# Lists of places made in pieces behind the table chunks, place loads split from their subtraction, and transposed rows kept in the tiles of the sums

## The chip, the core and the metric

The kernel runs on one core of a Trainium2 chip. The core has five engines that run their own instruction streams and meet at semaphores: PE (TensorE, the matrix unit), DVE (VectorE), ACT (ScalarE), POOL (GpSimd, here used to start gathers of table rows) and SP (SyncE, here used to start transfers). ACT also starts transfers. Sixteen DMA engines move the data between the memory of the chip and the on-chip buffers SBUF and PSUM. The metric is the device time of one execution in microseconds (us); lower is better.

## The reference

One step of message passing on a graph with 12,500 nodes of 64 values and 200,000 edges of 32 values. The edges are sorted by destination.

```python
msg_in = jnp.concatenate([nodes[row], nodes[col], edge_features], axis=-1)
messages = relu(msg_in @ mW1 + mb1) @ mW2 + mb2
aggregated = jax.ops.segment_sum(messages, col, num_segments=nodes.shape[0])
upd_in = jnp.concatenate([nodes, aggregated], axis=-1)
x = layernorm(x + relu(upd_in @ uW1 + ub1) @ uW2 + ub2)
```

`row` is the source of an edge and `col` its destination. The hidden width is 128.

## The kernel before, in words

The first matrix mW1 is split into the rows for the source, for the destination and for the edge values. Two tables are made once, A = x times the source rows and B = x times the destination rows, both with 12,500 rows of 128 values in the memory of the chip. An edge then needs one row of A (its source), one row of B (its destination) and a small product of its 32 own values.

**Opening: 13 chunks.** Table A is made in 13 chunks of 8 blocks of 128 nodes (the last has 2 blocks). For chunk k, `chunk_a` lets PE multiply the blocks into a PSUM buffer `pb`; ACT copies one half of it to an SBUF tile `tb` (L656), DVE the other half (L654), and ACT then starts the store of `tb` to table A (L658). There are two `pb` buffers and four `tb` buffers, so PE can start chunk k+2 when both halves of chunk k are copied, and the copies of chunk k+4 wait until the store of chunk k has landed. Between the chunks stand other pieces of work: one chunk of table B, the comparison masks of the first edge groups (`select_rows`, L273, and `select`, L281), and, behind chunk 10, `offsets()`. This function makes, on one partition, the lists of places at which the sums of each edge tile are to be added: `usup`, `woff`, `wcnt` and `ustep`, views of one tile `lists`. They are read by PE's sequencer in `collect`, from step 1 on. POOL starts gathers during the chunks: 48 gathers of rows of x for the first eight steps (a batch of four is held until ACT has copied the chunk ahead of it), and gathers of table A only after all 13 stores have landed.

**The steps.** The edges are worked in 261 steps of 6 tiles of 128 edges. In step s, PE adds the source rows to a PSUM tile `pc` (`node_part`), ACT or DVE applies relu into `h`, PE adds the counts and the messages of step s-1 into the running sums (`collect`, L486 and L490), and makes the part of the destinations and edge values of step s+1 (`edge_part`, L410). `pc` takes the same two PSUM buffers that the chunks used as `pb`. For the first eight steps the source rows come from x itself, not from table A: PE transposes them (`transpose`, L326) into one PSUM tile `pt`, ACT copies them to a tile `xt` (L327) and `node_part` multiplies them by the source matrix (L429). `xt` is a buffer of the same rotation of four as `tb`. From step 8 on rows of table A are gathered and added (L437). The order of instructions on each engine is the order in which the program is written; nothing reorders it.

**Relative places.** In steps 1, 2 and 3 `rest(s)` calls `relative(a, b)`: SP starts a load of 512 columns of destinations (`dst`, L599) and of the first destination of each tile (`wrow`, broadcast to all partitions into `col_a`, L600), and DVE subtracts one from the other (L601) into `drc`. `col_a` is one buffer, so the second load waits for the first subtraction. `drc` beyond its first 96 columns is read by `select` from step 13 on.

**Tiles of the sums.** `sums_s[0]` and `sums_s[1]` are two SBUF tiles that take the finished sums of a stretch of nodes; the first of them is written behind step 44, where the first stretch of 45 steps ends.

Of the kernel before, what the change touches and what calls it, by code (L numbers as in the profile page):

```python
# [10 lines left out]
F32 = mybir.dt.float32  # L11
I32 = mybir.dt.int32
AF = mybir.ActivationFunctionType
ALU = mybir.AluOpType
# [3 lines left out]
P = 128  # L18
# [5 lines left out]
NT = -(-E // P)  # L24
SUB = 6
SUP = 12
NSUP = -(-NT // SUP)
NTP = NSUP * SUP
# [44 lines left out]
U8 = mybir.dt.uint8  # L73
YBASE = XBASE + 4 * XCOLS
LEAD = 8
SBASE = (33556480, 33554432)
CBASE = 33566720
PACE = ((11, 0.48), (50, 0.505), (130, 0.483), (170, 0.469), (261, 0))
# [49 lines left out]
def gnn_kernel(ctx: ExitStack, tc: tile.TileContext, x1T, x, eT, e_rows, src, src_row, dst, dst_row, wlist, wrow, wnext, whalf,  # L128
# [117 lines left out]
    with tc.tile_pool(name="work", bufs=2) as work, tc.manual_schedule():  # L246
# [74 lines left out]
        def transpose(s):  # L321

            a = xg.pop(s)[1]
            xt = work.tile([P, SUB // 2, P], F32, name="xt", tag="tb", bufs=4)
            for k in range(SUB // 2):
                nc.tensor.transpose(pt[:, k, :], a[:, 2 * k:2 * k + 2].rearrange("p k d -> p (k d)"), ident)  # L326
            nc.scalar.copy(xt, pt)  # L327
            xs[s] = xt
# [264 lines left out]

        WCH = 512

        def relative(a, b):

            wbc = col_a.rearrange("p a e b -> p (a e b)")[:, :b - a]
            nc.sync.dma_start(dst_s[:, a:b], dst[:, a:b])  # L599
            nc.sync.dma_start(wbc, wrow[:, a:b].broadcast_to([P, b - a]))  # L600
            nc.vector.tensor_tensor(drc[:, a:b], dst_s[:, a:b], wbc, op=ALU.subtract)  # L601

        def halves(a, b):

# [64 lines left out]
        def offsets():  # L669

            nc.vector.memset(usup[:, 0:1], 0)
            wv = wint.rearrange("o (s t) -> o s t", t=LS)
            ov = woff.rearrange("o (s t) -> o s t", t=LS)
            k, runs = 0, []
            while k < K:
                end = UPD[k + 1:] + [NSUB]
                d = end[0] - UPD[k]
                n = 1
                while k + n < K and k and end[n] - UPD[k + n] == d:
                    n += 1  # L680
                if k:
                    nc.vector.tensor_copy(usup[:, k:k + n], wv[:, UPD[k]:UPD[k] + (n - 1) * d + 1:d, 0])
# [4 lines left out]
                k += n  # L687
            nc.vector.tensor_tensor(ustep[:, 1:], usup[:, 1:], usup[:, :-1], op=ALU.subtract)
            for v in (woff[:, :NSUB * LS], ustep[:, 1:]):
                nc.vector.tensor_scalar(v, v, 0.0, float(UN), op0=ALU.max, op1=ALU.min)  # L690
            v = woff[:, :NSUB * LS]
            nc.vector.tensor_scalar(wcnt[:, :NSUB * LS], v, 4.0, float(CBASE), op0=ALU.mult, op1=ALU.add)
            nc.vector.tensor_scalar(v, v, 4.0, float(SBASE[0]), op0=ALU.mult, op1=ALU.add)
            for k, d, n in runs:
                if k % 2 == 0:
                    k, n = k + 1, n - 1
                if n > 0:
                    o = ov[:, UPD[k]:UPD[k] + n * d].rearrange("o (n d) t -> o n (d t)", n=n)[:, ::2]
                    nc.vector.tensor_scalar(o, o, float(SBASE[1] - SBASE[0]), None, op0=ALU.add)

        dst_s = drc.bitcast(I32)
        nc.scalar.dma_start(src_s[:, :64], src[:, :64])
# [32 lines left out]
        for r in rhs:  # L735
            for o in EK:
                nc.sync.dma_start(r[o:o + DE], mW1[2 * D:, :].unsqueeze(1).broadcast_to([DE, SUP // 2, DH]))
        for k, c in enumerate(range(0, NB, NCH)):
            copied = chunk_a(c)
            for i, u in enumerate(first[:EACH]):  # L740
                fetch(u, None if i else copied)
            first = first[EACH:]
            if k == 2:
                chunk_b(0, [B0v, Bv])
            if k == 3:
                nc.vector.tensor_tensor(drc[:, :8 * SUP], dst_s[:, :8 * SUP], early, op=ALU.subtract)
                first_nodes(0, 8)
            if k == 4:

                w0 = wint[:, :GE * SUP // SUB * LS]  # L750
                nc.vector.tensor_scalar(past, w0[:, GE * SUP // SUB * LS - 1:], float(EARLY - WIN), None, op0=ALU.is_gt)
                nc.vector.tensor_scalar(w0, w0, float(EARLY - WIN), None, op0=ALU.min)
                windows(0)
                windows(1)
            if k in (5, 7):
                g = (k - 5) // 2
                select_rows(g)
                load(g)
                select(g)
                counts(g)  # L760
            if k == 10:
                offsets()
        assert not first

        def rest(s):
# [370 lines left out]
```

## Time and profile before

| what | value |
|---|---|
| runs of the kernel (three) | 2145.4, 2143.6, 2152.13 us |
| median | 2145.4 us |
| profiled execution, whole time | 2147.86 us |
| its span from first to last instruction | 2146.1 us |
| mean granted TensorE clock | 0.778 |
| opening until PE starts the first step | 80.09 us |
| PE starts the node part of step 15 at | 213.47 us |
| from there to the end of the span | 1932.53 us |

Rows of the timeline give the start in us, the duration in us, the engine, the source line, the operation, output and input, the number of merged instructions, and in brackets the idle time of the engine just before and what ended it. `ACTq` and `SPq` rows are starts of transfers. "issue" means that the engine waited for nothing that the profile shows, "remote" that the release is not among the instructions shown. The ends of matrix multiplications are modelled. A row of the view by stretches gives, for each engine, busy time and number of instructions, then the granted clock of PE, the share of the DMA engines and the transfer rate.

### The profile page before, as it was taken

The page shows a single profiled execution, that of the slowest core. Times are in us where ns is not written, and L with a number is a line of the kernel's source. Part 1 is how long each engine was busy: PE and PEld are TensorE (multiplying, and loading weights), DVE is VectorE, ACT ScalarE, POOL GpSimd, SP SyncE. Part 2 cuts the span into 40 slices and gives each one's busy share as a digit, 9 for nine tenths or more (in the row PEclk, how much of TensorE's full clock was granted, in tenths as well). Part 3 has the DMA queues.
Part 4 walks back from the last instruction along what each step waited for, and adds up shares of the span by engine and source line. Part 5 has one row for each costly group of instructions (what it writes and reads, how often), then busy time and mean ns, then how long its engine had stood idle before and what let it go on. Part 6 is the DMA issues. An engine that isn't in the chain of part 4 may idle for free. (4 is left out here: it accounts for less than half of the span.)

```text
span 2146.1 us, 47795 instructions
## 1 busy us (share of the span) xinstructions
PE 1692.0 (79%) x10742; PEld 1284.5 (60%) x10742; DVE 1135.8 (53%) x8047; ACT 1575.1 (73%) x8029; POOL 1257.7 (59%) x1336
## 2 busy tenths in 40 slices
PE   3476877888778887878887887888887888888888
PEld 3454665666555665656565656556665666666666
DVE  2414555565555555565555645565555565555553
ACT  1155988769869697889677877787877877878872
POOL 6565666665666666555656655565656666666650
PEclk8667877777787778787877777787788787878788
DMA  8452333332222222232223323233333333333331
GB/s 221 114 138 73 104 89 97 89 92 74 78 74 78 75 79 79 76 85 78 76 81 83 89 75 88 81 94 83 81 89 85 84 96 85 92 86 94 85 89 40
DMA packets 207836, 190.41 MB, mean 89 GB/s; under 512 B 57909, under 2 KB 174093, under 8 KB 207549
## 3 DMA queue, kind: packets, MB, share of 16 engines
q0 software_dynamic: 42464, 85.48, 16.0%
q1 hardware_dynamic: 150396, 92.86, 15.5%
q10 hardware_dynamic: 14690, 8.99, 1.5%
q8 instruction: 90, 1.47, 0.3%
q14 instruction: 196, 1.61, 0.2%
HBM read 169.15 MB, written 18.02 MB: 87 GB/s over the span
## 5 line engine op out<-in xcount | busy, mean ns | idle before, releaser
L239 POOL DMA_INDIRECT xg<-tab_a,src_s x1279 | 1211.0, 947 | 806.7 <-issue 264.7
L381 ACT ACTIVATE xc<-xtop,xbot 128x1 f32 x7872 | 1491.8, 293 | 163.6 <-issue 118.8
L389 DVE TENSOR_TENSOR xc<-xtop,xbot 128x1 int32 x7232 | 607.0, 155 | 470.6 <-issue 455.4
L490 PE MATMUL sums<-band,h 128*128 128x96 f32 x3126 | 539.2, 327 | 144.0 <-issue 88.4
L490 PEld LDWEIGHTS sums<-band,h 128*128 128x128 f32 x3126 | 476.8, 233 | 174.3 <-issue 103.4
L437 PE MATMUL pc<-xg,band 128*128 128x384 f32 (+1 forms) x1008 | 451.5, 574 | 31.8 <-issue 26.7
L410 PE MATMUL pc<-rhs,l 64*128 64x128 f32 x3126 | 371.5, 351 | 89.7 <-issue 66.3
L410 PEld LDWEIGHTS pc<-rhs,l 64*128 64x128 f32 x3126 | 291.8, 234 | 140.5 <-issue 97.5
L450 DVE TENSOR_SCALAR h<-pc 128x768 f32<-128x768 f32 x252 | 240.3, 953 | 197.2 <-PE sums L490 69.5
L437 PEld LDWEIGHTS pc<-xg,band 128*128 128x128 f32 x1008 | 216.4, 237 | 148.8 <-issue 96.3
L273 DVE TENSOR_TENSOR l<-l,cps 128x768 f32<-128x768 int32 (+1 forms) x134 | 127.1, 948 | 146.0 <-PE pc L437 66.8
L486 PEld LDWEIGHTS <-one 128*1 128x1 bf16 x1563 | 56.5, 81 | 215.3 <-issue 211.0
L561 ACT ACTIVATE y<-cps 128x256 f32<-128x256 f32 (+1 forms) x36 | 13.7, 382 | 179.8 <-issue 86.9
L486 PE MATMUL cnt<-band,one 128*1 128x32 bf16 x1563 | 89.6, 180 | 42.2 <-issue 40.9
L544 ACT ACTIVATE hTu<-sums,ub_s 128x416 f32<-128x416 f32 (+1 forms) x36 | 21.7, 603 | 96.0 <-PE pc L437 23.8
L413 PE MATMUL pc<-band,xc 64*128 64x128 f32 x472 | 77.6, 313 | 17.3 <-issue 16.7
L281 DVE TENSOR_TENSOR band<-cps,drc 128x384 f32<-128x384 f32 x131 | 71.7, 547 | 22.1 <-remote 14.9
L646 PE MATMUL pb<-band,xtop 64*128 64x128 f32 x200 | 43.7, 386 | 41.8 <-DVE tb L654 27.2
L413 PEld LDWEIGHTS pc<-band,xc 64*128 64x128 f32 x472 | 64.0, 228 | 15.5 <-issue 15.4
L646 PEld LDWEIGHTS pb<-band,xtop 64*128 64x128 f32 x200 | 38.3, 281 | 46.7 <-DVE tb L654 28.6
L239 POOL DMA_INDIRECT xg<-in_x,src_s x48 | 45.7, 952 | 24.3 <-issue 13.1
L552 PE MATMUL cps<-ux,xw 128*128 128x64 f32 x284 | 54.3, 347 | 5.2 <-issue 5.0
(107 smaller groups left out, 657.5 us busy)
## 6 DMA issues: line engine op xcount, KB each, us to landing
l<-in_dst_row SPq DMA_DIRECT2D x262, 96.0 KB
l<-in_eT SPq DMA_DIRECT2D x262, 96.0 KB
xg<-tab_a,src_s POOLq DMA_INDIRECT x1279
rhs<-tab_b SPq DMA_DIRECT2D x361, 32.0 KB
tab_b<-tb SPq DMA_DIRECT2D x13, 512.0 KB
rhs<-tab_b SPq DMA_DIRECT2D x387, 16.0 KB
tab_a<-tb ACTq DMA_DIRECT2D x12, 512.0 KB
out<-y SPq DMA_DIRECT2D x35, 128.0 KB
```

The source lines that it names most:

```text
L239: ins = nc.gpsimd.indirect_dma_start(out=a[:, i, :] if s < XG else a[:, i // 2, i % 2, :], out_offset=None, in_=A[:, :] if s >= XG else x[ ...
L273: nc.vector.tensor_tensor(l[r], l[r].bitcast(I32), node[r].unsqueeze(2).broadcast_to([r.stop - r.start, SUP // 2, P]), op=ALU.is_equal)
L281: nc.vector.tensor_tensor(s[:, :nt], slot.unsqueeze(1).broadcast_to([P, nt, WIN]), drc[:, g * SUP:g * SUP + nt].unsqueeze(2).broadcast_to( ...
L381: nc.scalar.activation(o[:, e:e + 1], top.bitcast(F32), AF.Identity, bias=bot.bitcast(F32))
L389: nc.vector.tensor_tensor(o[:, e:e + 1].bitcast(I32), top.bitcast(I32), bot.bitcast(I32), op=ALU.bitwise_or)
L410: done = nc.tensor.matmul(pc[:, b, k, :], L[g][q:q + 64, m, :], rhs[g % 2][q:q + 64, w, :], start=k == 0, stop=False)
L413: done = nc.tensor.matmul(pc[:, b, k, :], xc[s][q:q + 64], w1a[q:q + 64], start=False, stop=False)
L437: added = nc.tensor.matmul(pc[:, b, :m], ident, a[:, b, :m], start=False, stop=True)
L450: nc.vector.tensor_scalar(h, pc, 0.0, None, op0=ALU.max)
L486: nc.tensor.matmul(pn8[:, bass.ds(cs[i] - CBASE, 4 * WIN)].bitcast(F32), one, SB[g][:, k0 + i, :, 1], start=False, stop=ends and i == n - 1)
L490: made.append(nc.tensor.matmul(ps8[:, bass.ds(ws[i] - SBASE[u % 2], 4 * WIDE * WIN)].bitcast(F32), h[:, i % 2, i // 2, :], widened(g, k0 + i),
L646: nc.tensor.matmul(pb[:, h, i, :], (xbot if h else xtop)[64 * h:64 * h + 64, (c + HB * h + i) * P:(c + HB * h + i + 1) * P], w[64 * h:64 * ...
```

## The change

Three edits, all in the opening and the first eight steps.

1. `offsets()` becomes a generator that yields after each piece, and behind each of the chunks 5 to 12 up to four pieces are taken. The pieces are the same instructions in the same order.
2. `relative` is split. `absolute_load` starts the two loads in steps 1, 3 and 5; `relative`, now only the subtraction, runs in steps 3, 5 and 7, ahead of the next load into the same buffer.
3. `transpose` writes its copy into `sums_s[s % 2]` instead of a buffer of the rotation that the table chunks use.

```diff
+OFFS = 4
 def transpose(s):
     a = xg.pop(s)[1]
-    xt = work.tile([P, SUB // 2, P], F32, name="xt", tag="tb", bufs=4)
+    xt = sums_s[s % 2][:, :SUB // 2 * P].rearrange("p (k n) -> p k n", n=P)
...
+def absolute_load(a, b):
+    nc.sync.dma_start(dst_s[:, a:b], dst[:, a:b])
+    nc.sync.dma_start(col_a.rearrange("p a e b -> p (a e b)")[:, :b - a], wrow[:, a:b].broadcast_to([P, b - a]))
 def relative(a, b):
-    wbc = col_a.rearrange("p a e b -> p (a e b)")[:, :b - a]
-    nc.sync.dma_start(dst_s[:, a:b], dst[:, a:b])
-    nc.sync.dma_start(wbc, wrow[:, a:b].broadcast_to([P, b - a]))
-    nc.vector.tensor_tensor(drc[:, a:b], dst_s[:, a:b], wbc, op=ALU.subtract)
+    nc.vector.tensor_tensor(drc[:, a:b], dst_s[:, a:b], col_a.rearrange("p a e b -> p (a e b)")[:, :b - a],
+                            op=ALU.subtract)
...
 # in offsets(): a yield after each run of stretches, after ustep, after each clamp,
 # after wcnt, after woff, and after every fourth of the last additions
...
+places_made = offsets()
 for k, c in enumerate(range(0, NB, NCH)):
     copied = chunk_a(c)
...
-    if k == 10:
-        offsets()
+    if k > 4:
+        for _ in range(OFFS):
+            next(places_made, None)
+for _ in places_made:
+    pass
...
-    if 1 <= s < 4:
-        relative(8 * SUP + (s - 1) * WCH, min(8 * SUP + s * WCH, NT))
-        if s == 2:
-            halves(4 * SUP, NTP // 2)
+    for stage, a in ((relative, s - 3), (absolute_load, s - 1)):
+        if a in (0, 2, 4):
+            stage(8 * SUP + a // 2 * WCH, min(8 * SUP + (a // 2 + 1) * WCH, NT))
+    if s == 2:
+        halves(4 * SUP, NTP // 2)
```

Where the lists stand on DVE, before: `tb_356`, `tb_373` and `tb_390` are the halves of chunks 8, 9 and 10, and the whole of `offsets()` begins behind them.

```order
L654 COPY tb_356<-pb_347 128x512
L654 COPY tb_373<-pb_364 128x512
L654 COPY tb_390<-pb_381 128x512
L671 MEMSET usup_104 1x1
L684 TENSOR_TENSOR lists_69<-lists_69,usup_104 1x360
L682 COPY usup_104<-lists_69 1x1
```

The same place on DVE after the change: `tb_380` and `tb_401` are the halves of chunks 8 and 9.

```order
L688 TENSOR_TENSOR lists_69<-lists_69,usup_104 1x48
L658 COPY tb_380<-pb_371 128x512
L693 TENSOR_TENSOR ustep_105<-usup_104 1x35
L696 TENSOR_SCALAR lists_69<-lists_69 1x2088
L696 TENSOR_SCALAR ustep_105<-ustep_105 1x35
L699 TENSOR_SCALAR lists_69<-lists_69 1x2088
L658 COPY tb_401<-pb_392 128x512
L701 TENSOR_SCALAR lists_69<-lists_69 1x2088
L708 TENSOR_SCALAR lists_69<-lists_69 1x152
```

The 12 differences (L688), which stood between chunks 10 and 11, are now behind chunks 5, 6 and 7, four behind each; four instructions stand behind chunk 8 and the last ten behind chunk 9, so that the halves of chunks 10 and 11 follow each other on DVE with nothing between.

On DVE in the first steps, before: the subtractions of `relative` (L601) stand behind the half of chunk 11 (`tb_441`) and the masks of the third group, in the steps whose `rest` starts their loads.

```order
L654 COPY tb_441<-pb_432 128x512
L273 TENSOR_TENSOR l2_82<-l2_82,cps_101 32x768 x2
L281 TENSOR_TENSOR band_97<-cps_101,drc_102 128x384
L601 TENSOR_TENSOR drc_102<-drc_102,col_a_71 128x512 x2
L273 TENSOR_TENSOR l0_80<-l0_80,cps_101 128x768
```

The same stretch of DVE after the change: the subtractions are L604.

```order
L658 COPY tb_441<-pb_432 128x512
L274 TENSOR_TENSOR l2_82<-l2_82,cps_101 32x768 x2
L282 TENSOR_TENSOR band_97<-cps_101,drc_102 128x384
L274 TENSOR_TENSOR l0_80<-l0_80,cps_101 128x768
L282 TENSOR_TENSOR band_97<-cps_101,drc_102 128x384
L604 TENSOR_TENSOR drc_102<-drc_102,col_a_71 128x512
```

The first subtraction now stands behind the masks of the fourth group, two steps behind its own load, and the next two follow one group of masks later each. On SP the loads of the second and third pieces move from steps 2 and 3 to steps 3 and 5.

On ACT in the same stretch, before, with the semaphores that each instruction waits for (names with DMAHW count landed transfers):

```order
L656 COPY tb_448<-pb_445 128x256 [waits DMAHW7_49,PE_49]
L658 DMA tab_a_63<-tb_448 128x2x128 [waits DMAHW5_49,Activation_49]
L327 COPY xt_451<-pt_117 128x384 [waits DMAHW2_49,PE_49]
L431 ACTIVATE h_480<-pc_456 128x768 [waits PE_49]
L327 COPY xt_490<-pt_117 128x384 [waits DMAHW3_49,PE_49]
L431 ACTIVATE h_504<-pc_495 128x768 [waits PE_49]
L327 COPY xt_556<-pt_117 128x384 [waits DMAHW4_49,PE_49]
```

And after the change:

```order
L660 COPY tb_448<-pb_445 128x256 [waits DMAHW1_49,PE_49]
L662 DMA tab_a_63<-tb_448 128x2x128 [waits Activation_49]
L328 COPY sums_s0_73<-pt_117 128x384 [waits PE_49]
L432 ACTIVATE h_479<-pc_455 128x768 [waits PE_49]
L328 COPY sums_s1_74<-pt_117 128x384 [waits PE_49]
L432 ACTIVATE h_502<-pc_493 128x768 [waits PE_49]
L328 COPY sums_s0_73<-pt_117 128x384 [waits PE_49,Activation_49]
```

The copies of the transposed rows stand at the same places and no longer wait for a landed transfer. From step 10 on the order on all engines is the same as before.

More of the change, by code (lines that the diff above doesn't have):

```diff
@@ L687, in offsets @@
                 k += n
+                yield
             nc.vector.tensor_tensor(ustep[:, 1:], usup[:, 1:], usup[:, :-1], op=ALU.subtract)
+            yield
             for v in (woff[:, :NSUB * LS], ustep[:, 1:]):
                 nc.vector.tensor_scalar(v, v, 0.0, float(UN), op0=ALU.max, op1=ALU.min)
+                yield
             v = woff[:, :NSUB * LS]
             nc.vector.tensor_scalar(wcnt[:, :NSUB * LS], v, 4.0, float(CBASE), op0=ALU.mult, op1=ALU.add)
+            yield
             nc.vector.tensor_scalar(v, v, 4.0, float(SBASE[0]), op0=ALU.mult, op1=ALU.add)
+            yield
             for k, d, n in runs:
@@ L699, in offsets @@
                     nc.vector.tensor_scalar(o, o, float(SBASE[1] - SBASE[0]), None, op0=ALU.add)
+                    if k % 4 == 0:
+                        yield
         dst_s = drc.bitcast(I32)
```

## The prediction

> **What bounds the kernel now.** I read the page first, then the view by stretches, then the timeline of each engine over the opening.
>
> ```profile
> span 2146.1 us, 47795 instructions
> PE 1692.0 (79%) x10742; PEld 1284.5 (60%) x10742; DVE 1135.8 (53%) x8047; ACT 1575.1 (73%) x8029; POOL 1257.7 (59%) x1336
> ```
>
> ```profile
> 60.00:80.00 20.00, 4.99 (x39) 4.40 (x39) 13.89 (x42) 1.76 (x3) 9.01 (x10) 0.59 0.40 103
> ...
> 600.00:800.00 200.00, 163.12 (x977) 121.26 (x975) 111.21 (x862) 166.53 (x879) 121.71 (x129) 0.77 0.29 78
> ```
>
> Over the long run of steps PE and ACT are each over 80% busy (163.12 and 166.53 of 200 us), and PE at a granted clock of 0.77. The opening is another stage: in 60 to 80 us PE works 4.99 of 20 us, and DVE is the busiest engine with 13.89. The change touches only the opening and the first eight steps, so I look for what ends last there and ask how far a shift lasts.
>
> ACT and DVE between chunk 7 and the first steps:
>
> ```profile
> 56.16 0.59 ACT L656 COPY tb<-pb 128x512 f32<-128x512 f32 x1 [14.39 <-remote]
> ...
> 61.08 0.59 ACT L656 COPY tb<-pb 128x512 f32<-128x512 f32 x1 [2.53 <-DVE tb L654]
> ...
> 64.80 0.59 ACT L656 COPY tb<-pb 128x512 f32<-128x512 f32 x1 [3.13 <-PE pb L646]
> 66.14 0.37 ACTq L658 DMA_DIRECT2D tab_a<-tb  x1
> 74.08 0.59 ACT L656 COPY tb<-pb 128x512 f32<-128x512 f32 x1 [8.69 <-remote]
> 80.07 0.37 ACTq L658 DMA_DIRECT2D tab_a<-tb  x1
> 80.54 0.37 ACT L656 COPY tb<-pb 128x256 f32<-128x256 f32 x1 [5.87 <-DVE tb L654]
> 80.94 0.37 ACTq L658 DMA_DIRECT2D tab_a<-tb  x1
> 81.40 0.48 ACT L327 COPY xt<-pt 128x384 f32<-128x384 f32 x1 [0.49 <-ACT tb L656]
> ...
> 97.42 0.48 ACT L327 COPY xt<-pt 128x384 f32<-128x384 f32 x1 [9.27 <-remote]
> ```
>
> ```profile
> 41.81 0.69 DVE L654 COPY tb<-pb 128x512 f32<-128x512 f32 x1 [1.80 <-issue]
> 56.78 0.69 DVE L654 COPY tb<-pb 128x512 f32<-128x512 f32 x1 [14.28 <-ACT tb L656]
> ...
> 59.43 0.56 DVE L281 TENSOR_TENSOR band<-cps,drc 128x384 f32<-128x384 f32 x1
> 59.91 0.68 DVE L654 COPY tb<-pb 128x512 f32<-128x512 f32 x1
> 61.70 0.69 DVE L654 COPY tb<-pb 128x512 f32<-128x512 f32 x1 [1.11 <-issue]
> 65.42 0.69 DVE L654 COPY tb<-pb 128x512 f32<-128x512 f32 x1 [3.02 <-issue]
> 66.05 0.06 DVE L671 MEMSET usup<- 1x1 int32 x1
> ...
> 70.07 0.43 DVE L682 COPY usup<-lists 1x4 int32<-1x4 int32 x1
> ...
> 73.92 0.18 DVE L688 TENSOR_TENSOR ustep<-usup 1x35 int32<-1x35 int32 x1 [0.50 <-issue]
> ...
> 76.87 1.24 DVE L693 TENSOR_SCALAR lists<-lists 1x2088 int32<-1x2088 int32 x1
> ...
> 79.35 0.69 DVE L654 COPY tb<-pb 128x512 f32<-128x512 f32 x1
> ...
> 92.60 0.69 DVE L601 TENSOR_TENSOR drc<-drc,col_a 128x512 f32<-128x512 int32 x1 [10.01 <-issue]
> 97.22 0.69 DVE L601 TENSOR_TENSOR drc<-drc,col_a 128x512 f32<-128x512 int32 x1 [3.92 <-DMA col_a<-in_wrow]
> ...
> 118.28 0.62 DVE L601 TENSOR_TENSOR drc<-drc,col_a 128x443 f32<-128x443 int32 x1 [14.36 <-DMA col_a<-in_wrow]
> ```
>
> ```profile
> 57.53 0.58 PE L646 MATMUL pb<-band,xtop 64*128 64x128 f32 x1 [12.89 <-DVE tb L654]
> ...
> 60.64 0.58 PE L646 MATMUL pb<-band,xtop 64*128 64x128 f32 x1 [1.03 <-DVE tb L654]
> ...
> 62.51 0.51 PE L646 MATMUL pb<-band,xtop 64*128 64x128 f32 x1
> ...
> 80.09 1.65 PE L410 MATMUL pc<-rhs,l 64*128 64x128 f32 x12 [12.75 <-DVE tb L654]
> ...
> 89.79 0.49 PE L326 MATMUL pt<-band,xg 128*128 128x128 f32 x3
> ...
> 97.95 1.65 PE L429 MATMUL pc<-band,xt 64*128 64x128 f32 x12 [6.80 <-issue]
> ```
>
> ```profile
> 70.81 0.95 POOL L239 DMA_INDIRECT xg<-in_x,src_s  x1 [0.30 <-issue]
> 84.58 0.95 POOL L239 DMA_INDIRECT xg<-tab_a,src_s  x1 [12.82 <-DMA tab_a<-tb]
> ```
>
> DVE takes its half of chunk 10 at 65.42, works on the lists from 66.05 on, and takes its half of chunk 11 at 79.35. ACT's half of chunk 11 was copied at 74.08 to 74.67. ACT can't start the store before DVE is done (80.07), chunk 12 stands behind it (80.54, 80.94), PE's first step waits for the same PSUM buffer (80.09, 12.75 us idle ahead of it), and POOL waits 12.82 us for all stores until 84.58. So the lists hold the end of the opening, but only from 74.67 on: before that DVE would have waited for ACT, and ACT for something the profile calls remote (8.69 us).
>
> **The lists in pieces.** The instructions are the same; their time on DVE is 66.05 to 79.35, 13.3 us. By the rows above, the pieces behind chunks 5 and 6 end at 70.07 (4.0 us); those behind chunk 7 reach to 73.92 (3.85, with small idle times), behind chunk 8 to 76.87 (2.95), behind chunk 9 to 79.35 (2.5). The first 4.0 us are free: chunk 6's half ends at about 42.5 us, and DVE then idles 14.28 us ahead of 56.78. The rest stands between the halves of chunks 7 to 10. From DVE's 59.99 (end of the masks behind chunk 7): pieces to 63.8, chunk 8's half to 64.5 (60.6 before), pieces to 67.5, chunk 9's half to 68.1 (62.4 before), pieces to 70.6, chunk 10's half to 71.3 (66.1 before). So three stores start 4 to 6 us later, at 64.5, 68.1 and 71.3; nobody waits for these alone, since POOL needs all 13. ACT comes to chunk 11 at 71.8, by the 0.47 us from 80.07 to 80.54.
>
> When is chunk 11's product there for ACT? This the trace doesn't show, as the release at 74.08 has no name, so I bound it. Early end: PE's chunk 11 starts when chunk 9's half is copied (62.51 now, 68.2 then) and takes as long as chunk 10 did, from 60.64 to ACT's copy at 64.80, 4.2 us; that is 72.4, then 0.59 for ACT and 0.69 for DVE, and the store starts at 73.7, which is 6.4 us earlier than 80.07. Late end: it takes as long from its start as it did itself, 74.08 less 62.51, 11.6 us; that is 79.8, the store starts at 81.1, 1.0 us later than now. I take the time at which it came, 74.08: it lies between the two, and the wait ended 2.3 us after POOL's last gather of the opening (70.81 and 0.95), whose batch is released by chunk 7's copy (56.16), and that doesn't move. Then DVE's half ends at 75.4 and the store starts there: **4.6 us earlier**, with ends of 6.4 earlier and 1.0 later. PE's first step starts with it, and POOL's gathers of table A, by the 3.64 us from 80.94 to 84.58, at about 80.0.
>
> **The subtractions apart from their loads.** DVE waits 10.01, 3.92 and 14.36 us for these loads (rows 92.60, 97.22, 118.28). Behind it on DVE stand the masks of the groups that PE reads three steps later; SP's next loads wait for those masks:
>
> ```profile
> 93.32 0.33 SPq L600 DMA_DIRECT2D col_a<-in_wrow  x1
> ...
> 98.80 0.81 SPq L294 DMA_DIRECT2D l<-in_eT  x2
> ```
>
> The broadcast at 93.32 waited 4 us for the first subtraction; it goes. The edge values loaded at 98.80 belong to group 3, which is steps 6 and 7, and PE is then at the node part of step 2 (97.95), so what DVE and SP gain here ends as idle time. Nothing is late next: the three subtractions of 0.69, 0.69 and 0.62 us run in steps 3, 5 and 7, when their loads are long there, and are read from step 13 on. The same two times 256 KB per piece move, the second and third piece later. I count 0; if the transfers at 93 to 97 us slowed what PE waited for, it is part of the larger case below.
>
> **The transposed rows in the tiles of the sums.** The first copy at 81.40 follows chunk 12's store start by 0.46 us, so it hardly waited for a buffer. The third, at 97.42, waited 9.27 us, and PE with it (97.95; its transposes ran at 89.79 to 90.28). Its buffer was that of chunk 11's store. But POOL, which waits for that very store, went on at 84.58, so the store had landed 13 us before; I count 0 for this edit as well. Bounds: a gain of 97.42 less 90.28, 7.1 us, if the wait is the buffer's after all, and no loss, as the copy has the same shape and only waits for less.
>
> [...]
>
> **The sum.** 4.6 and 0 and 0: 4.6 us off 2147.86 gives 2143.3 us for the profiled execution. That execution is 2.46 us above the median of 2145.4, so I forecast **2140.8 us**. That the gain stays to the end I take from the code: from step 10 on all engines have the same order, no step waits for a fixed time, and each is released by the one before.
>
> **The rivals.**
> - *No lag at chunk 11.* ACT's wait for it goes with the new order, and the early end holds: 6.4 us, 2139.0. For it speak chunks 9 and 10 (57.53 to 61.08 and 60.64 to 64.80); against it that ACT had no work and still waited 8.69 us.
> - *The buffer was the wait.* The third copy runs at PE's pace: 4.6 and 7.1, 2133.7. For it speaks that the copy at 97.42 came 0.2 us after a transfer had landed for DVE (97.22); against it POOL's row.
> - *Slower: chunk 11 hangs on its own start.* The pieces behind chunks 7 and 8 push PE's start of chunk 11 from 62.51 to 68.2, and if it then needs 11.6 us the store starts at 81.1. This costs 1.0 us: 2146.4. It decides from a start of 67.2 on; the reckoning has 68.2. The 8.69 us without work between speak for a lag of PE, the 4.2 us of chunk 10 against it.
> - *Slower: the granted clock answers.* PE starts 4.6 us sooner and has fewer pauses, and is granted less. Clock rows of one run go from 0.59 to 0.77 by stretch. A hundredth of 0.77 over the 1692 us that PE is busy is 22 us, more than the whole gain; it decides from two thousandths on, and gives some 2163 with a hundredth. Against it: after step 10 the work is the same.
>
> **How the numbers follow.** Likeliest 0.46; no lag 0.12; the buffer 0.19; slower by chunk 11 0.15; slower by the clock 0.08. What a measurement can tell from no change I put at 0.5%, 10.7 us, from the spread of the three runs (2143.6 to 2152.13). Only the buffer's case passes it on the fast side (11.7 us) and the clock's on the slow side: faster 0.19, same 0.73, slower 0.08. The range holds the first four cases, with 2133.7 and 2146.4 as its ends, and some us for the spread of runs above: 2132 to 2149. What is left out is the clock's 0.08 and a part of the buffer's case.
>
> **What would show it.** Right: DVE's half of chunk 11 starts straight behind ACT's, at about 74.7; the store at 75.4; POOL's first row of table A at 80; no L604 with more than 1 us of idle ahead; the third transposed copy still some 7 us behind its transposes. Wrong: chunk 11's copy on ACT at 79 or 72; the third copy at once behind PE; steps 15 to 260 taking another time than the 1932 us between 213.47 and the end. If ACT's unnamed waits in the opening move with the order, the whole sum moves with them.

## The result, and the profile after

The changed kernel takes 2139.93 us (median of 20 runs, 2133.43 to 2144.39), the kernel before 2148.48 us (median of 20 runs on the same chip). The ratio is 0.9962 with a 95% interval of 0.9951 to 0.9972; of 2148.48 us that is 8.2 us faster, between 6.0 and 10.5. The profiled execution of after took 2141.37 us, 6.5 us less than that of before.

The head of the page of after:

```profile
span 2139.6 us, 47801 instructions
PE 1688.8 (79%) x10742; PEld 1279.5 (60%) x10742; DVE 1134.1 (53%) x8047; ACT 1572.4 (73%) x8029; POOL 1256.0 (59%) x1336
```

The same stretches as shown of before; columns as there:

```profile
60.00:80.00 20.00, 13.82 (x112) 11.40 (x113) 11.31 (x22) 5.18 (x9) 11.15 (x10) 0.63 0.54 152
600.00:800.00 200.00, 159.77 (x970) 119.44 (x970) 111.53 (x856) 168.09 (x886) 121.13 (x129) 0.76 0.28 77
```

In 60 to 80 us PE is now busy for 13.82 us instead of 4.99: the first steps have moved into this stretch. The long run of steps is as before, with a granted clock of 0.76 (0.77 before).

ACT from chunk 8 to the first steps, the timeline of after:

```profile
61.60 0.59 ACT L660 COPY tb<-pb 128x512 f32<-128x512 f32 x1 [13.61 <-remote]
...
67.10 0.58 ACT L660 COPY tb<-pb 128x512 f32<-128x512 f32 x1 [3.11 <-DVE tb L658]
...
70.68 0.58 ACT L660 COPY tb<-pb 128x512 f32<-128x512 f32 x1 [2.99 <-issue]
72.02 0.37 ACTq L662 DMA_DIRECT2D tab_a<-tb  x1
...
72.88 0.43 ACTq L662 DMA_DIRECT2D tab_a<-tb  x1
...
80.41 0.48 ACT L328 COPY sums_s<-pt 128x384 f32<-128x384 f32 x1 [1.87 <-PE pt L327]
91.80 0.81 ACT L432 ACTIVATE h<-pc 128x768 f32<-128x768 f32 x1 [10.92 <-PE pc L411]
```

DVE in the same kernel; L686 to L708 are the pieces of the lists, L604 the subtractions:

```profile
53.86 0.20 DVE L688 TENSOR_TENSOR lists<-lists,usup 1x48 int32<-1x48 int32 x1
62.22 0.69 DVE L658 COPY tb<-pb 128x512 f32<-128x512 f32 x1 [8.15 <-ACT tb L660]
62.83 0.17 DVE L693 TENSOR_TENSOR ustep<-usup 1x35 int32<-1x35 int32 x1
...
64.69 1.24 DVE L699 TENSOR_SCALAR lists<-lists 1x2088 int32<-1x2088 int32 x1
65.97 0.69 DVE L658 COPY tb<-pb 128x512 f32<-128x512 f32 x1
66.69 1.24 DVE L701 TENSOR_SCALAR lists<-lists 1x2088 int32<-1x2088 int32 x1
...
69.49 0.69 DVE L658 COPY tb<-pb 128x512 f32<-128x512 f32 x1
71.29 0.69 DVE L658 COPY tb<-pb 128x512 f32<-128x512 f32 x1 [1.11 <-ACT tb L660]
...
97.32 0.68 DVE L604 TENSOR_TENSOR drc<-drc,col_a 128x512 f32<-128x512 int32 x1
...
115.02 0.68 DVE L604 TENSOR_TENSOR drc<-drc,col_a 128x512 f32<-128x512 int32 x1
...
134.89 0.61 DVE L604 TENSOR_TENSOR drc<-drc,col_a 128x443 f32<-128x443 int32 x1
```

PE, the first matrix multiplication of chunk 11 and the first step, and POOL around the end of the opening:

```profile
66.71 0.58 PE L650 MATMUL pb<-band,xtop 64*128 64x128 f32 x1 [1.67 <-DVE tb L658]
...
72.22 1.65 PE L411 MATMUL pc<-rhs,l 64*128 64x128 f32 x12
```

```profile
63.70 2.36 POOL L240 DMA_INDIRECT xg<-in_x,src_s  x1 [0.31 <-issue]
66.36 1.69 POOL L240 DMA_INDIRECT xg<-in_x,src_s  x1 [0.30 <-issue]
...
78.25 0.94 POOL L240 DMA_INDIRECT xg<-tab_a,src_s  x1 [3.96 <-DMA tab_a<-tb]
```

Four things are to be seen. The pieces behind chunks 5 to 7 lie in DVE's idle time (they end at 54.06, chunk 8's half follows at 62.22). Chunk 11 is copied by ACT at 70.68, 3.97 us after PE began it at 66.71, and the wait of 8.69 us ahead of it is gone; as ACT started the store of chunk 10 only at 70.21, chunk 11 needed 3.97 us at most. Its store starts at 72.02 instead of 80.07. POOL starts the gathers of table A at 78.25 instead of 84.58, 6.33 us earlier, and waits 3.96 us for the stores instead of 12.82. And the place where ACT stalls has moved: the third transposed copy comes at once (80.41), but the next operation of ACT stalls 10.92 us, until 91.80.

How far the shift lasts is read from PE's node parts of steps 8 and 15:

```profile
141.01 1.56 PE L438 MATMUL pc<-xg,band 128*128 128x384 f32 x4
...
206.81 1.56 PE L438 MATMUL pc<-xg,band 128*128 128x384 f32 x4
```

PE starts the first step 7.87 us earlier (72.22 against 80.09) and the node part of step 15 6.66 us earlier (206.81 against 213.47). From there to the end of the span it is 1932.8 us, before it was 1932.5, so the gain is made ahead of step 15. From POOL's first gather of table A to the end it is 2146.1 less 84.58 = 2061.5 us before and 2139.6 less 78.25 = 2061.4 us after. That these agree to 0.1 us is in part chance, since single executions of the changed kernel lie up to 11 us apart. Which of the two earlier starts carries the gain, PE's first step or POOL's first gather of table A, these rows do not tell: both follow the end of the opening. The rows of table A for step 8 were asked for by 84.49 and are added at 141.01, so the first steps did not wait for them.

### The profile page after: what moved, and what is told of

It is laid out like the page before. It is cut to its first block, busy times and chain, and to the rows that moved or that the text cites. A ratio compares the mean times of both kernels' runs of the same rounds, so it can differ in the third digit from the quotient of the medians.

```text
span 2139.6 us, 47801 instructions
## 1 busy us (share of the span) xinstructions
PE 1688.8 (79%) x10742; PEld 1279.5 (60%) x10742; DVE 1134.1 (53%) x8047; ACT 1572.4 (73%) x8029; POOL 1256.0 (59%) x1336
## 5 line engine op out<-in xcount | busy, mean ns | idle before, releaser
L438 PE MATMUL pc<-xg,band 128*128 128x384 f32 (+1 forms) x1008 | 456.5, 578 | 36.1 <-issue 33.8
L555 PE MATMUL cps<-u2c,hTu 128*128 128x64 f32 x284 | 53.3, 337 | 6.7 <-issue 6.7
```

The costliest lines, as they stand in the source:

```text
L438: added = nc.tensor.matmul(pc[:, b, :m], ident, a[:, b, :m], start=False, stop=True)
```

## The experiments

The experiments ran on chips of two kinds of pace: on some the kernel before takes 2174 us, near the 2148 us of the prediction's chip, on others 1690 us. Each run is compared with the kernel before on its own chip.

### One edit at a time, and the lists in one piece at another place (a chip with 1690.55 us)

Each of the first three kernels is before with one edit of the change; the fourth is before with one line changed.

```diff
 # lists in pieces alone (with the yields in offsets())
-            if k == 10:
-                offsets()
+            if k > 4:
+                for _ in range(OFFS):
+                    next(places_made, None)
 # subtractions alone
-                relative(8 * SUP + (s - 1) * WCH, min(8 * SUP + s * WCH, NT))
+            for stage, a in ((relative, s - 3), (absolute_load, s - 1)):
 # transposed rows alone
-            xt = work.tile([P, SUB // 2, P], F32, name="xt", tag="tb", bufs=4)
+            xt = sums_s[s % 2][:, :SUB // 2 * P].rearrange("p (k n) -> p k n", n=P)
 # lists whole, behind chunk 6
-            if k == 10:
+            if k == 6:
                 offsets()
```

> Only the first edit: the lists in pieces; the subtractions and the transposed rows as before. Theory of the prediction (the lists hold the end of the opening, the other two edits cost and bring nothing): the whole gain of the change is here, 6 to 10 us (the two medians are 8.6 us apart), and POOL's first gather of table A starts at 77 to 80 us instead of 84.58. Rival (the buffer of the transposed rows, or the subtractions, bring part of it): at most 4 us here, and the rest in the other two kernels.

> Only the second edit: the subtractions apart from their loads. Theory of the prediction: DVE's idle time of 10.01, 3.92 and 14.36 us ahead of the three subtractions goes and nothing else does; 0 us, at most 1 either way, and POOL's first gather of table A stays at 84 to 85 us. Rival (SP's wait of 4 us at 93.32, or the transfers of 256 KB at 86 to 97 us, held up PE's steps 2 and 3): 2 to 5 us faster, with the third transposed copy on ACT 2 to 5 us earlier than 97.42.

> Only the third edit: the transposed rows in the tiles of the sums. Theory of the prediction: the wait of 9.27 us ahead of the third transposed copy was not for its buffer; the copy stays at 95 to 99 us, or another instruction of ACT or PE stalls until then; 0 us, at most 1 either way. Rival (the buffer was the wait): the third copy follows its transposes, at about 90.5 instead of 97.42, and the time falls by up to 7 us.

> The kernel before with the lists made in one piece, but behind chunk 6 instead of chunk 10; nothing else is changed. Theory (the place counts, not the pieces): DVE's idle time of 14.28 us ahead of its half of chunk 7 takes the 13.3 us in; nothing stands between the halves of chunks 7 to 11 any more; gain as with the pieces or 1 to 3 us more (7 to 11 us), POOL's first gather of table A at 75 to 80 us. Rival (the pieces count): the lists in one piece push DVE's half of chunk 7 back, from 56.78 to as much as 58, or by the whole 13 us where ACT's stall of 14.39 us has moved away from chunk 7; the gain is under 4 us, or there is a loss.

| kernel | median, us | ratio to before, 95% interval |
|---|---|---|
| lists in pieces alone | 1688.35 | 0.9985 (0.9974 to 0.9995) |
| subtractions alone | 1691.48 | 1.0009 (1.0001 to 1.0018) |
| transposed rows alone | 1689.51 | 0.9996 (0.9988 to 1.0005) |
| lists whole, behind chunk 6 | 1689.94 | 0.9999 (0.9989 to 1.0009) |

None of it is worth 6 us here. The lists in pieces bring 2.2 us, the subtractions cost 0.9, the other two stay within their intervals; the expectation of 6 to 10 us for the lists and of 7 to 11 for their place was wrong on this chip. POOL's timeline of the lists alone and of the transposed rows alone tells why:

```profile
64.69 0.94 POOL L240 DMA_INDIRECT xg<-in_x,src_s  x1 [0.30 <-issue]
65.94 0.94 POOL L240 DMA_INDIRECT xg<-tab_a,src_s  x1 [0.30 <-issue]
```

```profile
64.03 0.95 POOL L239 DMA_INDIRECT xg<-in_x,src_s  x1 [0.30 <-issue]
65.42 0.94 POOL L239 DMA_INDIRECT xg<-tab_a,src_s  x1 [0.45 <-issue]
```

POOL goes from the last gather of x to the first of table A with 0.30 or 0.45 us between them: it has no time in which it waits for the stores. With the lists in one piece behind chunk 10 or in pieces the first gather of table A starts at 65.42 and 65.94 us. An earlier end of the stores has nobody to release; the 2.2 us of the lists are not explained by these rows. The pages show that this is so for the whole kernel. POOL's gathers of table A, with their count, busy time, mean ns and the idle time ahead of them, first of before on the prediction's chip, then of the lists alone on this one:

```profile
L239 POOL DMA_INDIRECT xg<-tab_a,src_s x1279 | 1211.0, 947 | 806.7 <-issue 264.7
```

```profile
L240 POOL DMA_INDIRECT xg<-tab_a,src_s x1279 | 1208.8, 945 | 389.9 <-issue 253.9
```

Here the 389.9 us are 0.30 us ahead of each gather on average: gathers and gaps fill 1598.7 of the 1620.2 us behind the first of them, and POOL sets the pace from the first gather of table A to the last. On the prediction's chip POOL idles 806.7 us and waits for others in the steps.

From table A's first gather to the end of the span it is 1620.2 us with the lists alone and 1621.7 with the transposed rows alone.

### The whole change on another chip (2173.62 us)

> The changed kernel, all three edits, once more. The four kernels before it ran on a chip on which the kernel before takes 1690.55 us, not 2148: there POOL issues its gathers one behind the other, every 1.25 us, from 24 us on, and its first gather of table A starts at 65.4 to 65.9 us in all four, with the lists in one piece or in pieces. Theory (what the change is worth hangs on whether POOL waits for the stores): on such a chip 0 to 3 us, as the lists in pieces alone (2.2 us); on a chip on which the kernel before takes some 2148 us, 6 to 10 us again, with POOL's first gather of table A at 77 to 80 us. Rival (the gain is the same whatever the chip): 6 to 10 us on either.

2166.19 us against 2173.62; ratio 0.9964 (0.9946 to 0.9983). So the result repeats on a second chip of the slower pace. POOL's and ACT's timelines of this execution:

```profile
78.89 0.94 POOL L240 DMA_INDIRECT xg<-tab_a,src_s  x1 [4.02 <-DMA tab_a<-tb]
```

```profile
71.25 0.59 ACT L660 COPY tb<-pb 128x512 f32<-128x512 f32 x1 [2.99 <-issue]
...
87.03 0.48 ACT L328 COPY sums_s<-pt 128x384 f32<-128x384 f32 x1 [6.36 <-remote]
```

Table A's first gather and chunk 11's copy stand within 0.7 us of where they stood in the profile of after (78.25, 70.68); chunk 11 has no stall again.

### The edits apart on a third chip of that pace (2174.14 us)

The first kernel is the lists in pieces alone again. The second is the change without its first edit, so before with both of these:

```diff
-                relative(8 * SUP + (s - 1) * WCH, min(8 * SUP + s * WCH, NT))
+            for stage, a in ((relative, s - 3), (absolute_load, s - 1)):
...
-            xt = work.tile([P, SUB // 2, P], F32, name="xt", tag="tb", bufs=4)
+            xt = sums_s[s % 2][:, :SUB // 2 * P].rearrange("p (k n) -> p k n", n=P)
```

The third is the lists whole behind chunk 6 once more.

> The first edit alone again, meant for a chip on which the kernel before takes some 2150 to 2170 us; two of the chips so far were such, one was not (1690 us). Theory (the stores' end releases POOL there, and the lists held the stores): the whole gain of the change, 6 to 10 us, POOL's first gather of table A at 77 to 80 us. Rival (the transposed rows or the subtractions bring a part): under 4 us here, and the rest in the next kernel. On a chip with some 1690 us: 0 to 3 us, as on the first.

> The second and the third edit together, without the first: the lists in one piece behind chunk 10. Theory: 0 us, at most 1.5 either way; POOL's first gather of table A at 83 to 86 us; ACT or PE still stall until some 97 us in the first steps, at the third transposed copy or the instruction behind it. Rival (the buffer was the wait): the third copy and all behind it come up to 7 us sooner, and the time falls by 3 to 7 us.

> The lists in one piece behind chunk 6, nothing else changed. Theory (the place counts, not the pieces): on a chip with some 2150 us ACT's long stall of the opening (14 to 17 us ahead of the copy of chunk 7 or 8) covers the lists; gain as with the pieces or up to 3 us more, 6 to 12 us. Rival (the pieces count): under 4 us or a loss, because the lists in one piece hold DVE's half of chunk 7 back by up to 13 us where the stall stands elsewhere. On the chip with 1690 us it was 0.6 us.

| kernel | median, us | ratio to before, 95% interval | PE's first step, us | table A's first gather, us | node part of step 15, us |
|---|---|---|---|---|---|
| lists in pieces alone | 2167.33 | 0.9966 (0.9950 to 0.9981) | 72.83 | 78.99 | 210.78 |
| subtractions and transposed rows | 2175.30 | 1.0007 (0.9996 to 1.0019) | 86.43 | 90.91 | 220.16 |
| lists whole, behind chunk 6 | 2171.41 | 0.9975 (0.9962 to 0.9988) | 76.01 | 80.50 | 209.59 |

The first edit alone has the ratio of the whole change (0.9966 against 0.9962 and 0.9964), the other two together have none. Some expectations missed: in the second kernel table A's first gather was to start at 83 to 86 us and started at 90.91, and the stall of the first steps was to end at some 97 us and ended at 104.28; the third kernel was to gain 6 to 12 us and gained 2.7. The rows that bear on the transposed rows, the third copy on ACT: first with the lists alone, where it still takes a buffer of the chunks' rotation, then with the two other edits, where it goes to the tiles of the sums.

```profile
86.88 0.48 ACT L328 COPY xt<-pt 128x384 f32<-128x384 f32 x1 [6.12 <-remote]
```

```profile
72.69 0.58 ACT L659 COPY tb<-pb 128x512 f32<-128x512 f32 x1 [14.86 <-remote]
...
74.44 0.59 ACT L659 COPY tb<-pb 128x512 f32<-128x512 f32 x1 [1.16 <-remote]
...
86.87 0.37 ACT L659 COPY tb<-pb 128x256 f32<-128x256 f32 x1 [11.84 <-DVE tb L657]
...
104.28 0.48 ACT L327 COPY sums_s<-pt 128x384 f32<-128x384 f32 x1 [9.74 <-remote]
```

In its new place the third copy still waits 9.74 us, and with all three edits it stood at 87.03 with 6.36 us, against 86.88 and 6.12 us with the lists alone. The wait was not for the buffer. The rows at 74.44 and 86.87 show the lists on the path, whole behind chunk 10: ACT copied its half of chunk 11 at 74.44, and idled 11.84 us until DVE had come to the other half. In this execution the stall and the lists stand one behind the other, and table A's first gather comes 11.9 us after that of the lists alone. At step 15 the difference is 9.4 us and at the end of the spans 7.4 (2174.8 and 2167.4); whether a part of the delay is made up, two single executions do not tell, as the runs of one kernel lie up to 11 us apart here.

The whole lists behind chunk 6 (their last nine operations, the half behind them, ACT and POOL):

```profile
56.60 1.18 DVE L699 TENSOR_SCALAR lists<-lists 1x152 int32<-1x152 int32 x9
57.81 0.69 DVE L654 COPY tb<-pb 128x512 f32<-128x512 f32 x1
```

```profile
56.70 0.59 ACT L656 COPY tb<-pb 128x512 f32<-128x512 f32 x1 [13.77 <-remote]
...
74.65 0.59 ACT L656 COPY tb<-pb 128x512 f32<-128x512 f32 x1 [9.36 <-remote]
```

```profile
80.50 0.95 POOL L239 DMA_INDIRECT xg<-tab_a,src_s  x1 [8.23 <-DMA tab_a<-tb]
```

ACT's stall of 13.77 us covers the lists almost wholly: DVE's half starts at 57.81, 0.52 us after ACT's copy has ended. But ACT stalls 9.36 us ahead of chunk 11, until 74.65, and POOL starts at 80.50. That is the picture that the prediction had drawn for the pieces (74.08 and 80.0), and it brings 0.25% (0.12 to 0.38). With the lists in pieces the late stall is gone in all three profiles of this pace (chunk 11 at 70.68, 71.25 and 71.29); with the lists whole it stands in all three (74.08 and 74.65 ahead of chunk 11, 72.69 ahead of chunk 10). So with the pieces two things are seen: the lists are gone from the end of the opening, and that stall is gone too. That the pieces are what ends it is read from three executions against three, and not shown. Nor is it shown that the pieces gain more than the place alone. The medians are 4.1 us apart, but the intervals overlap, and at step 15 the kernel with the lists whole behind chunk 6 is 1.2 us ahead (209.59 against 210.78), although its first step starts 3.2 us later.

### What takes the stall away: three kernels, on chips with 1690 us

```diff
 # gathers in twos: the changed kernel with
+ROOM = (4, 4, 4) + (2,) * 10
-            for i, u in enumerate(first[:EACH]):
+            for i, u in enumerate(first[:ROOM[k]]):
...
 # long operations: the lists whole behind chunk 6, and
+            if k in (8, 9):
+                for _ in range(2):
+                    nc.vector.tensor_scalar(lists[96:97, :NSUB * LS], wcnt[:, :NSUB * LS], 4.0, 0.0, op0=ALU.mult, op1=ALU.add)
 # masks: the same with
+                for _ in range(5):
+                    select(0)
```

> The changed kernel with the gathers of x spread: behind chunks 3 to 12 two are started with each chunk, not four, and the last eight behind chunk 12. Theory (ACT's stalls without a name are PE's counts that come late while a long run of POOL's gathers is under way; they ended 1 to 3 us behind each run: run to 53.2, copy at 56.16; run to 71.8, copy at 74.08): on a chip with some 2150 us the run of 16 gathers becomes one of 8, the stall ahead of chunk 7 or 8 ends 8 to 11 us sooner, chunk 12 is copied at 60 to 66 us, POOL's first gather of table A starts at 72 to 77 us although eight gathers of x now stand ahead of it, and the time falls by 9 to 14 us against the kernel before. Rival (the stalls do not hang on POOL's runs): chunk 7 or 8 is copied at 55 to 62 us as in the other kernels, the eight gathers come on top, table A's first gather starts at 82 to 85 us, and the time is that of before or up to 3 us more. On a chip with some 1690 us POOL has no pause to lose, and the spread costs 0 to 8 us.

> The lists in one piece behind chunk 6, and behind chunks 8 and 9 two more operations each on 2088 list values into an unused row (about 1.25 us each, their results are not used). Theory A (the long list operations hold POOL's gathers up, 2.36 and 1.69 us instead of 0.95, and with that PE's counts come in time): ACT's stall ahead of chunk 11 (9.36 us in the kernel without them) goes, chunk 11 is copied at 69 to 72 us, POOL's first gather of table A starts at 76 to 79 us: 1 to 3 us faster than the lists behind chunk 6 alone, although DVE does more. Theory B (it is the later start of PE's chunk 11 that takes it out of the stall, whatever DVE does meanwhile): the same here, and also in the next kernel. Rival (neither): chunk 11 at 74 to 80 us, table A at 80 to 86 us, 0 to 6 us slower than the lists behind chunk 6 alone.

> The same as the kernel before it, with five repetitions of the masks of the first group (0.56 us each) in place of the two long operations behind chunks 8 and 9: the halves are pushed back by about the same 2.5 us each, but POOL's gathers beside such masks took 0.95 us in the trace of before. Theory A: the stall stays, chunk 11 at 74 to 80 us, table A's first gather at 80 to 86 us, 0 to 6 us slower than the lists behind chunk 6 alone. Theory B: the stall goes as in the kernel before it, chunk 11 at 69 to 72 us, table A at 76 to 79 us.

> The changed kernel with the gathers of x in twos behind chunks 3 to 12, once more, meant for a chip with some 2150 us. What is open: ACT's wait of 8.69 us ahead of chunk 11 was to stay by the prediction; it is gone in the changed kernel and still there with the lists behind chunk 6. Theory (PE's counts come late while a long run of POOL's gathers is under way, and the long list operations broke the run): the stall ahead of chunk 7 or 8 ends 8 to 11 us sooner, chunk 12 at 60 to 66 us, table A's first gather at 72 to 77 us, 9 to 14 us faster than before (ratio 0.9935 to 0.996). Rival (the stalls do not hang on POOL's runs; PE's later start of chunk 11 took it out of the wait): chunk 7 or 8 at 55 to 62 us, table A's first gather at 82 to 85 us, ratio 0.9995 to 1.0015. On a chip with some 1690 us: 2 us slower, as before.

| kernel | median, us | before, us | ratio to before, 95% interval |
|---|---|---|---|
| gathers in twos | 1693.10 | 1690.91 | 1.0011 (1.0003 to 1.0020) |
| long operations | 1692.66 | 1690.91 | 1.0012 (1.0002 to 1.0023) |
| masks | 1690.52 | 1690.91 | 0.9992 (0.9980 to 1.0004) |
| gathers in twos, again | 1692.82 | 1690.51 | 1.0013 (1.0004 to 1.0022) |

All four ran on chips of the pace on which none of the first four kernels has such a stall (no wait of ACT's copies from 22 to 61 us is marked remote), so they do not tell the two theories of chunk 11 apart; that stays open. They show what ends the opening on these chips. PE's first step and POOL's first gather of table A with the gathers in twos (second run):

```profile
55.26 1.65 PE L412 MATMUL pc<-rhs,l 64*128 64x128 f32 x12
```

```profile
69.60 0.94 POOL L241 DMA_INDIRECT xg<-tab_a,src_s  x1 [0.30 <-issue]
```

PE starts 4.75 us sooner than in the kernel with the transposed rows alone (60.01), table A's first gather 4.18 us later (69.60 against 65.42), and the kernel is 0.13% slower than before, 2.3 us. This agrees with POOL's gathers standing one behind the other to the end: its later start costs, PE's earlier one brings nothing. The whole change itself was not measured on a chip of this pace, so the comparison is with before and with the third edit alone. POOL beside the four added list operations:

```profile
51.87 1.40 POOL L239 DMA_INDIRECT xg<-in_x,src_s  x1 [0.30 <-issue]
53.57 1.66 POOL L239 DMA_INDIRECT xg<-in_x,src_s  x1 [0.30 <-DMA xg<-in_x,src_s]
55.54 2.27 POOL L239 DMA_INDIRECT xg<-in_x,src_s  x1 [0.30 <-issue]
...
68.09 0.94 POOL L239 DMA_INDIRECT xg<-tab_a,src_s  x1 [0.30 <-issue]
```

Three gathers take 1.40, 1.66 and 2.27 us instead of 0.94, together 2.5 us more. Table A's first gather starts at 68.09, 2.7 us later than with the lists behind chunk 6 alone on a chip of that pace (65.40), and the median is 1.75 us above before. With masks in their place the median stays within 0.4 us of before, although POOL then waits for the stores on this chip too, and starts table A's gathers 1.1 us later than at 65.40:

```profile
66.52 0.94 POOL L239 DMA_INDIRECT xg<-tab_a,src_s  x1 [1.46 <-DMA tab_a<-tb]
```

## Why the prediction was right, and where it was wrong

**The sum.** Forecast were 2140.8 us and measured 2139.93. That it came within 0.9 us is luck, for two errors meet in this. The gain was put at 4.6 us and is 8.2 by the medians, 6.3 by POOL's row; and the median of three runs from which it was taken off, 2145.4, lies 3.1 us below the median of 20. (The times in the prediction give 80.07 less 75.4, 4.7 us; it wrote 4.6.)

**The lists in pieces: the mechanism right, a term mis-sized.** That the lists held the end of the opening, and PE's first step and POOL behind it, is shown: the first edit alone has the whole gain, and both come earlier with it. The step that failed is "I take the time at which it came, 74.08": chunk 11 was to reach ACT as late as before, whatever moved ahead of it. It came 3.97 us after its start on PE, which is the early end (4.2 us, as chunk 10). The reason given for 74.08 failed in the same trace: POOL's last gather of x was not to move, but it did, from 70.81 to 73.35, since the long stall now stands ahead of chunk 8 (until 61.60) and not of chunk 7 (until 56.16); and chunk 11 was copied at 70.68, while these gathers still ran. The rival "no lag at chunk 11", with a chance of 0.12 and a price of 6.4 us, is what happened; by POOL's row it was 6.33. The store of chunk 11 itself came 8.05 us earlier, but the last landing then took longer: from chunk 12's store to POOL 5.37 us (72.88 to 78.25), not 3.64. The kernel with the lists whole behind chunk 6 shows that the likeliest case was a real one: there the stall stays and POOL starts at 80.50. What was not seen is that the stall could go with the new order; what ended it stays open. The three stores ahead of it start at 62.94, 66.69 and 70.21 us, forecast were 64.5, 68.1 and 71.3.

**A cost that was left out.** "The instructions are the same" holds for DVE, not for POOL beside it: the gathers at 63.70 and 66.36 take 2.36 and 1.69 us instead of 0.94, 2.2 us together. In this kernel POOL then still waits 3.96 us for the stores, which covers it. On a chip with 1690 us, where POOL has no such pause, two gathers of 2.35 and 1.67 us stand beside the lists in one piece as well (the transposed rows alone, at 54.40 and 57.06), so there the pieces do not add this cost.

**The subtractions apart from their loads.** Counted at 0, and right: no L604 has idle time ahead of it any more (the idle time now stands one operation earlier, ahead of the masks: 16.31, 12.36 and 14.42 us), and with the transposed rows the ratio is 1.0007 (0.9996 to 1.0019).

**The transposed rows.** Counted at 0, and right, for the reason given: the wait at 97.42 was not for the buffer. The sign named for it was wrong, though. In the changed kernel the third copy follows at once, which was to speak for the buffer; the stall had moved to the instruction behind it (91.80). With the copy in the tiles of the sums no store is waited for, and with the second and third edits together 9.74 us of wait still stand ahead of it (104.28); so that wait was not for a store.

**The other rivals.** Chunk 11 hanging on its own start (slower, 0.15): it was started at 66.71, below the 67.2 from which it would have decided, and needed 3.97 us at most, not 11.6. The clock's answer (0.08): 0.774 against 0.778, and from step 15 to the end it is 1932.8 us against 1932.5. The buffer (0.19): ruled out by the two edits without the first.

**The bound of 0.5%.** It was taken from the spread of three runs. With 20 runs each the interval is 0.2% wide, so that 0.4% is told from nothing; "same" by the bound is a small gain in truth.

## What to carry to other kernels

Before pricing an edit in an opening, find the engine that sets the pace of the long run behind it, and ask whether the edit lets it start sooner on this chip. On the chips with 1690 us that is POOL, whose gathers of table A start at the same time with the edit and without it (65.94 and 65.42 us), and the edit is worth 2 us; on the slower chips POOL waits for others (806.7 us ahead of these gathers in before), the first step waits for the end of the opening, and the edit is worth 7 to 8. A wait whose releaser the profile does not name is no fixed time: it can move to another instruction or go when the order ahead of it changes (here 8.69 us ahead of chunk 11 went, and 9.27 us ahead of the third copy became 10.92 us ahead of the operation behind it), so its early end belongs in the likeliest case's range with more than a small chance. Work that is spread over gaps on one engine can hold up a neighbour (two gathers of 2.36 and 1.69 us instead of 0.94), so read the neighbour's durations beside it too.

## What was not expected of the hardware

**Two paces of chip.** The same kernel takes 2148 and 2174 us on some chips and 1690 us on others. The mean granted clock of the profiled executions is 0.77 to 0.78 on the first and 0.88 to 0.89 on the others. In the middle of the opening it was the same low one in these two, before (2148 us) and the lists alone (1690 us):

```profile
40.00:60.00 20.00, 4.16 (x32) 3.57 (x32) 3.86 (x7) 1.76 (x3) 12.51 (x14) 0.51 0.49 134
```

```profile
40.00:60.00 20.00, 12.85 (x93) 10.83 (x95) 17.61 (x40) 3.78 (x7) 15.67 (x15) 0.50 0.87 247
```

PE is granted 0.51 and 0.50 here, yet it does 32 matrix multiplications in the one and 93 in the other, so it is not the clock that makes this part longer. Two kernels on one chip with 1690 us say the same: in 40 to 60 us PE does 54 matrix multiplications in either, at a granted 0.50 with the long operations and at 1.00 with the masks. What makes it longer is not settled.

**PE's counts arrive late, and together.** In the traces of before and after ACT's stalls without a name ahead of the chunks end when counts of PE's semaphore arrive: an event of it stands 0.02 or 0.03 us ahead of each of the eight copies (20.15, 32.53, 41.19, 56.16 and 74.08 of before, 20.20, 38.06 and 61.60 of after), though ahead of 32.53 and 20.20 a landed transfer's stands as near. In the trace of before its events from 64 to 83.9 us stand as follows (the trace keeps 1835 of them, and 1982 matrix multiplications raise this semaphore):

```
64.77  74.05  74.11  74.14  74.18  74.21  83.61
```

PE's rows put the work behind the first six of them between 60.64 and 67.4 us; five of the six come between 74.05 and 74.21. The long stalls in the later part of the opening ended shortly behind a run of POOL's gathers:

| kernel | end of POOL's run, us | ACT's copy, us | between, us |
|---|---|---|---|
| before | 53.2 | 56.16 | 3.0 |
| before | 71.8 | 74.08 | 2.3 |
| after | 58.8 | 61.60 | 2.8 |
| after, on the other chip | 53.3 | 56.88 | 3.6 |
| lists in pieces alone | 59.3 | 62.37 | 3.0 |
| subtractions and transposed rows | 71.0 | 72.69 | 1.7 |
| lists whole, behind chunk 6 | 55.4 | 56.70 | 1.3 |
| lists whole, behind chunk 6 | 72.3 | 74.65 | 2.4 |

Against it stands that other stalls ended in the middle of a run. In after the one of 10.92 us ended at 91.80, while POOL's gathers ran from 78.25 to 94.2:

```profile
90.74 0.94 POOL L240 DMA_INDIRECT xg<-tab_a,src_s  x1 [0.30 <-issue]
91.99 0.94 POOL L240 DMA_INDIRECT xg<-tab_a,src_s  x1 [0.30 <-PE pc L411]
```

With the lists whole behind chunk 6 a stall of 5.29 us ended at 42.34, inside a run from 33.72 to 55.4. On the chips with 1690 us POOL's runs go on without such stalls: with the lists alone no gap between gathers from 23.70 to 65.94 us is over 0.31 us, and no wait of ACT from 22 us to its first transposed copy is marked remote. That the runs hold the counts back is therefore not shown. POOL's next gathers also wait for that very copy (3.83 us ahead of 57.02 in before, 3.62 us ahead of 62.45 in after, both ended by ACT's copy), so a run ends because ACT stalls. The kernel that would tell, with the gathers in twos, was not measured on a chip with stalls.

**Long list operations and gathers.** The gather at 63.70 of after ends at 66.06, 0.13 us after the list operation at 64.69 (to 65.93), and the one at 66.36 ends at 68.05, 0.12 us after that at 66.69 (to 67.93). The masks and the halves beside the gathers leave them at 0.94 or 0.95 us (of after, those at 50.41 and 72.10 beside masks, 62.45 and 69.60 beside halves). The kernels with long operations and with masks say the same: with four list operations added behind chunks 8 and 9 three gathers from 51.87 on take 1.40, 1.66 and 2.27 us, and with masks in their place none from 46.63 to 64.11 takes over 0.95. What makes the gathers longer no row shows.
